# Residual sums joined to VectorE's written order in a convolution-and-attention block, and one softmax sum moved from GpSimd to VectorE

## The chip, the cores and the metric

The kernel runs on one core of a Trainium2 chip. The metric is the device time of one execution in microseconds (us), of which the median over the runs is taken. TensorE (PE in the profile) multiplies matrices, VectorE (DVE) and ScalarE (ACT) do elementwise work, GpSimd (POOL) a part of it, and SyncE (SP) issues the DMAs. Each engine works through its own instructions strictly in the order of the program, and waits where an operand or a buffer is not ready.

## The reference

Eight images of 512 channels and 32x32 positions, all in fp32. `cbs` is a convolution, a batch norm with given statistics and SiLU; `gn` is a group norm with 32 groups.

```python
def block(x):                                  # C = 256 channels, 4 heads of 64
    t = cbs(x, cv1)                            # 1x1, 512 -> 512
    ys = [t[:, :C], t[:, C:]]
    for i in range(2):
        yi = ys[-1]
        z = cbs(yi, m_cv1[i], 3x3)             # 256 -> 256
        z = bot_attention(z, m_qkv[i], rw[i], rh[i])   # over all 1024 positions
        z = silu(bn(conv1x1(z, m_cv2[i])))     # 256 -> 256
        ys.append(yi + z)
    return cbs(concatenate(ys), cv2)           # 1x1, 1024 -> 512

x = x + block(gn(x))
x = x + last(gn(x))      # 1x1, 512 -> 512; weights scaled, masked and permuted by group tables
```

The attention is a softmax of `q . (k + r) / 8` with `r` the sum of two learned position terms, and the weighted sum of `v`.

## The kernel before

**Data.** A tile has 128 partitions; an image's 256 channels are two such tiles, and its 1024 positions two halves of 512. Activations between stages go through DRAM: `y_dram[n][0..3]` are the four parts that conv2 concatenates, `x2_dram[n]` is the image after the block's residual.

**The attention in units.** The work is cut into 16 slots (one image's block `i`), in the order image 0 block 0, image 1 block 0, image 0 block 1, image 1 block 1, and then the next two images. A slot has four units (`Unit`, 64 in all, called by image, block, pair of heads and half of the queries: the last one is 7_1_1_1). A unit works on eight tiles `t` of 128 keys for two heads, 128x1024 numbers each:

- `logits(t)`: TensorE makes the logits (L510) in two PSUM banks `lg`, ScalarE copies them to SBUF as `st` (L517), and VectorE keeps the running maximum `mx` out of the banks (L522). A bank is free for another product when both are done.
- `top` and `spread`: the maximum over the keys, transposed and negated (L531) and spread again over PSUM (`mb`, L539).
- `soften(t)`: VectorE adds `mb` to `st` (L544, 128x1024).
- `exponent(t)`: ScalarE takes the exponential of `st` in place (L548). From `t` = 1 on, GpSimd adds it to the sum of exponentials `sum_...` in four parts of 128x256 (L555).
- `values(t)`: TensorE multiplies the exponentials by `v` into `po` (L562).
- `finish` and `divide`: TensorE sums `sum_...` over the partitions (`den`, L576), ScalarE copies it (L579), VectorE takes the reciprocal (L583) and scales `po` into `q` (L585).

While one unit takes its exponentials and weighted sums, the next one's logits are made.

**Filler.** Between the steps of the units a generator (`slot_filler`) emits all other work of that time in pieces: `conv3` (the 3x3 convolution as six row products on transformed rows, `plane` tiles, L313), `project` (q, k, v), `conv_m2` (the 1x1 convolution behind the attention), and, from a list `bg` of items, `conv1`, `conv2` and `last` of other images. Its matmuls have L175 (`accumulate`). The emission keeps a clock of estimated time, `Clock`: `clock.at(delay, f)` calls `f` when that clock has moved on by `delay`; group norms and row transforms are placed with it.

**Order.** The order of emission becomes the order of an engine only where an instruction goes through `in_turn` (VectorE), `act_turn` (ScalarE) or `pe_turn` (TensorE); each ties the instruction to the one before it in its chain. VectorE's chain holds the maxima, the softens and some of the row transforms. The rest, the residual sums among them, is placed by the framework's scheduler where it finds room. DMAs are issued by SP (`load`, L78).

**The residual sums.** `conv_m2` works on the halves `h` and, in each, on two output tiles `co`, and so makes four sums a call, here called add 1 to add 4. For each half it loads the residual (`res`, 512 KB) from `y_dram`, makes the product, ScalarE applies batch norm and SiLU (`m2s`, L130), VectorE adds (L430) and SP stores the sum to `y_dram`. For block 0 the sum is written into `ybuf`, the input of the next 3x3 convolution; for block 1 in place. `conv2` does the same for four output tiles of each half: SiLU (`cv2s`), add to the image's `x` (`xr`, L457), statistics of the group norm (L139), and after every second one a store to `x2_dram`. The residual tiles of `conv_m2`, `conv2` and `last` (`res`, `xr`, `x2r`) come from one pool, `gr`, with two buffers; the SiLU outputs from `tp` with three. The PSUM banks of all these products and of the logits are five (`ps_f`).

The group norm of `x2` ends in small ops on 128x4 numbers: `gm_b` and `gv_b` on TensorE (L146, L156), `gd_b` on VectorE (L150 to L152), `gr_b` on GpSimd (L160), and then it is applied by ScalarE (L165) to the tiles that `last` reads.

Of the kernel before, what the change touches and what calls it, by code (L numbers as in the profile page):

```python
# [17 lines left out]
ALU = mybir.AluOpType  # L18
# [7 lines left out]
IT = 2  # L26
F = 32
HW = F * F
HALF = 512
# [10 lines left out]
def conv_preact_kernel(ctx: ExitStack, tc: tile.TileContext, x, cv1, cv2, mcv1, qkv, mcv2, bn, rw, rh, conv, s_in, t_in, out):  # L40
    nc = tc.nc
# [23 lines left out]
    def pair(p, tag, name):  # L65
        return p.tile([P, 2, HALF], F32, tag=tag, name=name)

    def bank(name):
        return ps_f.tile([P, HALF], F32, tag="bank", name=name)

    def half_tile(name):
        return tp.tile([P, HALF], F32, tag="t", name=name)

    def flat(t):
        return t.rearrange("p a b -> p (a b)")

    def load(dst, src):
        nc.sync.dma_start(out=dst, in_=src)  # L78

    def weights(name, shape, src):  # L80
        t = wp.tile([P, *shape], F32, tag="w", name=name)
        load(t, src)
        return t
# [12 lines left out]
    y_dram = [[dram.tile([P, IT, HW], F32, name=f"y_{n}_{j}") for j in range(4)] for n in range(NB)]  # L96
    x2_dram = [dram.tile([P, 2, CT, HALF], F32, name=f"x2_{n}") for n in range(NB)]
# [24 lines left out]
    def y_rows(c, h):  # L122

        return ybuf[:, c, 1 + 16 * h : 17 + 16 * h].rearrange("p r x -> p (r x)")
# [4 lines left out]
    def bn_silu(dst, src, col):  # L129
        nc.scalar.activation(dst, src, AF.Silu, bias=bn_b[:, col : col + 1], scale=bn_s[:, col : col + 1])  # L130


    class GroupNorm:
        def __init__(self, name):
            self.name = name
            self.st = small.tile([P, CT, 2, 6], F32, tag="st", bufs=3, name=f"st_{name}")
# [34 lines left out]
    def accumulate(ps, terms):  # L171


        for n, (w, moving) in enumerate(terms):
            nc.tensor.matmul(ps, w, moving, start=(n == 0), stop=(n == len(terms) - 1))  # L175
            if n % 2 and n < len(terms) - 1:
                yield 1.72
        return Whole(1.72)
# [3 lines left out]
    def in_turn(instruction):  # L182

        if turn:
            tc.add_manual_dep(instruction.ins, turn.pop().ins.name, IN_ORDER, reason="order of VectorE")
        turn.append(instruction)

    def act_turn(instruction):

        if act_last:  # L190
            tc.add_manual_dep(instruction.ins, act_last.pop().ins.name, IN_ORDER, reason="order of ScalarE")
        act_last.append(instruction)
# [11 lines left out]
    class Spread:  # L204
# [7 lines left out]
        def upto(self, n):  # L212
            while self.done < n:
                self.done += 1
                in_turn(self.ops[self.done - 1]())

    class Image:
        def __init__(self, n):
            self.n = n
# [196 lines left out]
        def conv_m2(self, i):  # L416
            n = self.n
            name = f"{n}_{i}"
            w = weights(f"w_m2_{name}", (IT, 256), mcv2[i])
            q = self.q  # L420
            for h in range(2):
                res = pair(gr, "gr", f"res_{name}_{h}")
                load(res, y_dram[n][1 + i][:, :, ts(h, HALF)])
                for co in range(IT):
                    ps = bank(f"m2_{name}_{co}_{h}")
                    us = yield from accumulate(ps, [(w[:, c, ts(co, P)], q[:, c, ts(h, HALF)]) for c in range(IT)])
                    t = half_tile(f"m2s_{name}_{co}_{h}")
                    bn_silu(t, ps, BN_M2 + IT * i + co)
                    dst = y_rows(co, h) if i == 0 else res[:, co]
                    nc.vector.tensor_tensor(dst, res[:, co], t, ALU.add)  # L430
                    load(y_dram[n][2 + i][:, co, ts(h, HALF)], dst)
                    yield us


# [8 lines left out]
        def conv2(self, h, ys):  # L443
            n = self.n
            if h == 0:
                self.gn1 = GroupNorm(f"b{n}")
            for cp in range(2):
                res = pair(gr, "gr", f"xr_{n}_{h}_{cp}")
                load(res, x[n, cp, :, :, ts(h, HALF)])
                for c in range(2):  # L450
                    co = 2 * cp + c
                    w = weights(f"w_cv2_{n}_{h}_{co}", (2 * CT, P), cv2[co])
                    ps = bank(f"cv2_{n}_{h}_{co}")
                    us = yield from accumulate(ps, [(w[:, k], ys[k // 2][:, k % 2]) for k in range(2 * CT)])
                    t = half_tile(f"cv2s_{n}_{h}_{co}")
                    bn_silu(t, ps, BN_CV2 + co)
                    nc.vector.tensor_tensor(res[:, c], res[:, c], t, ALU.add)  # L457
                    self.gn1.stats(co, h, res[:, c])
                    if c == 0:
                        yield us  # L460
                load(x2_dram[n][:, h, 2 * cp : 2 * cp + 2], res)
                yield us


        def load_x2(self, h):
# [27 lines left out]
    class Unit:  # L493
# [52 lines left out]
        def exponent(self, t):  # L546
            st = flat(self.st[t])
            act_turn(nc.scalar.activation(st, st, AF.Exp))  # L548
            if t == 1:
                self.acc = pair(one, "acc", f"sum_{self.name}")  # L550
            for j in range(4 if t else 0):

                part = slice(256 * j, 256 * j + 256)
                so_far = self.st[0] if t == 1 else self.acc
                nc.gpsimd.tensor_tensor(flat(self.acc)[:, part], flat(so_far)[:, part], st[:, part], ALU.add)  # L555
# [185 lines left out]
    units = [Unit(im, i, hp, half) for im, i in slots for hp in range(IT) for half in range(2)]  # L741

    class Clock:
# [18 lines left out]
        def flush(self):  # L762
            for _, f in sorted(self.due, key=lambda d: d[0]):
                f()
            self.due.clear()

    clock = Clock()
# [81 lines left out]
    class Background:  # L849
# [5 lines left out]
        def add(self, *items):  # L855
            self.items += items
# [294 lines left out]
```

## Time and profile before

| | |
|---|---|
| time, three runs | 3152.05, 3156.82, 3157.03 us; median 3156.82 us |
| the profiled execution | 3162.82 us, of which 3161.1 us are the span from the first to the last instruction |
| granted TensorE clock, mean | 0.996 of full speed |
| TensorE's waits for other engines, largest entry | 16.2 us, 14 times (weighted sum for an exponential) |
| VectorE's waits, largest entry | 433.2 us, 174 times (maximum for ScalarE's copy) |
| GpSimd's waits, largest entry | 1336.5 us, 287 times (sum for an exponential) |
| residual loads of `conv_m2` | 32 of 512 KB, median 4.0 us from issue to landing |

In the profile a line of a group reads: code line, engine, operation, output tile <- input tiles, shapes, count | busy time in us, mean ns of one | idle time of the engine ahead of them, and what ended it. A line of the timeline reads: start and duration in us, engine, code line, operation, tiles, shapes, count of instructions drawn together; in brackets the idle time before and what ended it. A line of the waits reads: who waited for whom, the total in us, how many times, the longest in us. A matmul of 128x512 in fp32 has two records on PE of about 0.43 us each.

### The profile page before, as it was taken

The page shows a single profiled execution, that of the slowest core. Times are in us where ns is not written, and L with a number is a line of the kernel's source. Part 1 is how long each engine was busy: PE and PEld are TensorE (multiplying, and loading weights), DVE is VectorE, ACT ScalarE, POOL GpSimd, SP SyncE. Part 2 cuts the span into 40 slices and gives each one's busy share as a digit, 9 for nine tenths or more (in the row PEclk, how much of TensorE's full clock was granted, in tenths as well). Part 3 has the DMA queues.
Part 4 walks back from the last instruction along what each step waited for, and adds up shares of the span by engine and source line. Part 5 has one row for each costly group of instructions (what it writes and reads, how often), then busy time and mean ns, then how long its engine had stood idle before and what let it go on. Part 6 is the DMA issues. An engine that isn't in the chain of part 4 may idle for free.

```text
span 3161.1 us, 34185 instructions
## 1 busy us (share of the span) xinstructions
PE 3077.0 (97%) x11668; PEld 1515.3 (48%) x11668; DVE 2049.9 (65%) x2718; ACT 1721.0 (54%) x2349; POOL 1398.4 (44%) x1867
## 2 busy tenths in 40 slices
PE   7999999998999999999999999999999999999999
PEld 3645354454445454455445454454445454453333
DVE  5446577567667576667666676767666676767642
ACT  3245765855655555644656455544656455546621
POOL 2104444546444554455444454445444464444520
PEclk9999999999999999999999999999999999999999
DMA  8852352421233232424233332424233332413356
GB/s 289 292 182 74 130 180 87 153 77 63 88 116 131 79 128 71 149 84 148 84 116 130 114 127 70 153 85 136 91 110 130 120 120 70 150 64 120 120 205 217
DMA packets 142014, 399.35 MB, mean 126 GB/s; under 512 B 13072, under 2 KB 14352, under 8 KB 141840
## 3 DMA queue, kind: packets, MB, share of 16 engines
q1 hardware_dynamic: 141120, 396.94, 36.6%
q8 instruction: 92, 1.51, 0.2%
q14 instruction: 82, 0.67, 0.1%
q10 hardware_dynamic: 720, 0.23, 0.0%
HBM read 317.42 MB, written 79.69 MB: 126 GB/s over the span
## 4 chain that ended last, share of the span: by engine, by line
PE 75%; DVE 4%; ACT 4%; issue 2%; DMA 1%; POOL 1%; SPq 0%; ACTq 0%; DVEq 0%; POOLq 0%
PE cv L175 15%; PE m L313 13%; PE po L562 12%; PE lg L510 12%; PE l L175 7%; PE qk L175 6%; PE v L405 3%; PE m L175 3%; PE den L576 2%; PE mb L539 2%; PE mt L530 1%; ACT st L517 1%; DVE st L544 1%; ACT st L548 1%; DVE mx L522 1%
## 5 line engine op out<-in xcount | busy, mean ns | idle before, releaser
L555 POOL TENSOR_TENSOR sum<-sum,st 128x256 f32<-128x256 f32 x1536 | 1132.0, 771 | 552.1 <-ACT st L548 547.7
L522 DVE TENSOR_TENSOR mx<-mx,lg 128x512 f32<-128x512 f32 x768 | 477.8, 682 | 417.6 <-ACT st L517 417.4
L517 ACT COPY st<-lg 128x512 f32<-128x512 f32 x1024 | 525.0, 597 | 356.1 <-PE lg L510 331.7
L548 ACT ACTIVATE st<-st 128x1024 f32<-128x1024 f32 x512 | 539.1, 1068 | 304.1 <-DVE st L544 302.9
L544 DVE TENSOR_TENSOR st<-st,mb 128x1024 f32<-128x1024 f32 x512 | 604.4, 1215 | 60.2 <-PE mb L539 60.2
L555 POOL TENSOR_TENSOR sum<-st,st 128x256 f32<-128x256 f32 x256 | 185.1, 754 | 788.8 <-ACT st L548 788.8
L313 PE MATMUL m<-plane,w_m 128*128 128x256 f32 x2304 | 528.8, 383 | 4.9 <-ACT cv2s L130 2.7
L562 PE MATMUL po<-st,v 128*64 128x512 f32 x2048 | 497.8, 605 | 18.2 <-ACT st L548 16.2
L510 PE MATMUL lg<-q,k 64*128 64x512 f32 x2048 | 510.9, 617 | 2.9 <-ACT y L130 2.9
L313 PEld LDWEIGHTS m<-plane,w_m 128*128 128x128 f32 x2304 | 426.4, 189 | 129.5 <-issue 45.1
L175 PE MATMUL cv<-y,w_cv 128*128 128x512 f32 x1024 | 464.5, 599 | 7.9 <-ACT cv2s L130 4.6
L510 PEld LDWEIGHTS lg<-q,k 64*128 64x128 f32 x2048 | 177.3, 186 | 328.2 <-issue 267.4
L175 PEld LDWEIGHTS cv<-y,w_cv 128*128 128x128 f32 x1024 | 185.8, 190 | 248.1 <-issue 226.4
L562 PEld LDWEIGHTS po<-st,v 128*64 128x64 f32 x2048 | 128.8, 136 | 323.6 <-issue 237.3
L175 PE MATMUL cv<-x,w_cv 128*128 128x512 f32 x512 | 237.0, 610 | 10.6 <-ACT y L130 3.7
L175 PE MATMUL l<-x,w_l 128*128 128x512 f32 x512 | 236.9, 606 | 7.9 <-DVE mx L522 6.9
L175 PE MATMUL qk<-z,w_qkv 128*128 128x512 f32 x512 | 234.0, 600 | 1.4 <-DVE mx L522 1.4
L583 DVE RECIPROCAL rb<-rb 128x256 f32<-128x256 f32 x128 | 215.5, 1723 | 26.0 <-ACT rb L579 25.8
L531 DVE TENSOR_REDUCE nm<-mt 128x4 f32<-128x512 f32 x128 | 82.3, 684 | 144.7 <-PE mt L530 144.7
L579 ACT COPY rb<-den 128x512 f32<-128x512 f32 x64 | 37.3, 583 | 230.4 <-PE den L576 230.4
L175 PEld LDWEIGHTS cv<-x,w_cv 128*128 128x128 f32 x512 | 95.3, 194 | 132.0 <-issue 109.3
L175 PEld LDWEIGHTS l<-x,w_l 128*128 128x128 f32 x512 | 93.4, 191 | 130.4 <-issue 112.2
(145 smaller groups left out, 2408.8 us busy)
## 6 DMA issues: line engine op xcount, KB each, us to landing
w_m<-w_m SPq DMA_DIRECT2D x96, 768.0 KB, 4.8
w_cv<-in_cv SPq DMA_DIRECT2D x90, 512.0 KB, 3.5
y<-y SPq DMA_DIRECT2D x64, 512.0 KB, 4.8
x<-in_x SPq DMA_DIRECT2D x56, 512.0 KB, 5.2
y<-y SPq DMA_DIRECT2D x64, 256.0 KB, 3.5
k<-r SPq DMA_DIRECT2D x32, 512.0 KB, 3.6
res<-y SPq DMA_DIRECT2D x32, 512.0 KB, 4.0
xr<-in_x SPq DMA_DIRECT2D x32, 512.0 KB, 4.1
```

The source lines that it names most:

```text
L175: nc.tensor.matmul(ps, w, moving, start=(n == 0), stop=(n == len(terms) - 1))
L313: nc.tensor.matmul(ps[:, ts(co, 256)].rearrange("p (t x) -> p t x", x=F), w[:, co, c, dx], u[:, 9 * c : 9 * c + 8, dx : dx + F], start=(j ...
L405: nc.tensor.matmul(ps[:, ts(j, P)], z[:, c, ts(4 * j4 + j, P)], w[:, c, 512 + P * hp : 512 + P * hp + P], start=(c == 0), stop=(c == IT - 1),)
L510: nc.tensor.matmul(lg[h], self.k[r, ts(t, P)], self.q[r, self.hp, ts(self.half, HALF)], start=True, stop=True)
L517: act_turn(nc.scalar.copy(st[:, h], lg[h]))
L522: in_turn(nc.vector.tensor_tensor(self.mx[:, h], so_far[:, h], lg[h], ALU.max))
L531: nc.vector.tensor_reduce(self.nm[:, h], mt, AX.X, ALU.max, negate=True)
L544: in_turn(nc.vector.tensor_tensor(st, st, flat(self.mb), ALU.add))
L548: act_turn(nc.scalar.activation(st, st, AF.Exp))
L555: nc.gpsimd.tensor_tensor(flat(self.acc)[:, part], flat(so_far)[:, part], st[:, part], ALU.add)
L562: nc.tensor.matmul(self.po[HD * h : HD * h + HD], self.v[:, t, ts(h, HD)], self.st[t][:, h], start=(t == 0), stop=(t == KT - 1),)
L583: nc.vector.reciprocal(self.rb[:, r], self.rb[:, r])
```

## The change

Three edits, and a helper class.

- `Later(delay)`: `add(f)` puts a function in a queue and asks the clock to run the queue up to it after `delay`; `flush()` runs what is left.
- `conv_m2`: the residual add and the store of its result are emitted through `Later(2.0)`, and the add goes through `in_turn`, so that it has a place in VectorE's chain. The queue is flushed with the last tile.
- `conv2`: the same with `Later(3.0)`; the add is in the chain, and the group norm's statistics and the store to `x2_dram` are emitted with it. One more `yield` is in the place of the one behind the store.
- `Unit.exponent`: for the last unit the sums of exponentials are seven VectorE adds of 128x1024 in the chain, in place of 28 GpSimd adds of 128x256.

```diff
+    class Later:
+        def __init__(self, delay):
+            self.delay, self.waiting = delay, []
+        def add(self, f):
+            self.waiting.append(f)
+            clock.at(self.delay, lambda: self.upto(f))
+        def upto(self, f):
+            while f in self.waiting:
+                self.waiting.pop(0)()
+        def flush(self):
+            if self.waiting:
+                self.upto(self.waiting[-1])
...
     conv_m2:
+            later = Later(2.0)
...
-                    nc.vector.tensor_tensor(dst, res[:, co], t, ALU.add)
-                    load(y_dram[n][2 + i][:, co, ts(h, HALF)], dst)
+                    def add(h=h, co=co, dst=dst, src=res[:, co], t=t):
+                        in_turn(nc.vector.tensor_tensor(dst, src, t, ALU.add))
+                        load(y_dram[n][2 + i][:, co, ts(h, HALF)], dst)
+                    later.add(add)
+                    if (h, co) == (1, IT - 1):
+                        later.flush()
                     yield us
...
     conv2:
+            later = Later(3.0)
...
-                    nc.vector.tensor_tensor(res[:, c], res[:, c], t, ALU.add)
-                    self.gn1.stats(co, h, res[:, c])
-                    if c == 0:
-                        yield us
-                load(x2_dram[n][:, h, 2 * cp : 2 * cp + 2], res)
-                yield us
+                    def add(cp=cp, c=c, co=co, res=res, t=t):
+                        in_turn(nc.vector.tensor_tensor(res[:, c], res[:, c], t, ALU.add))
+                        self.gn1.stats(co, h, res[:, c])
+                        if c == 1:
+                            load(x2_dram[n][:, h, 2 * cp : 2 * cp + 2], res)
+                    later.add(add)
+                    if (cp, c) == (1, 1):
+                        later.flush()
+                    yield us
...
     Unit.exponent:
+            if t and self is units[-1]:
+                so_far = self.st[0] if t == 1 else self.acc
+                in_turn(nc.vector.tensor_tensor(flat(self.acc), flat(so_far), st, ALU.add))
+                return
             for j in range(4 if t else 0):
```

## The prediction

> **What bounds the kernel now.** I read the page first, then TensorE's waits, then VectorE's groups of L430, then the timeline at the places that the change touches.
>
> ```profile
> PE 3077.0 (97%) x11668; PEld 1515.3 (48%) x11668; DVE 2049.9 (65%) x2718; ACT 1721.0 (54%) x2349; POOL 1398.4 (44%) x1867
> ```
>
> TensorE is busy for 3077.0 us of a span of 3161.1 us. Only 84 us can be won by any reordering, and a stall of TensorE anywhere is lost for good. Its waits, longest in total first:
>
> ```profile
> PE po L562 <- ACT st L548: 16.2, 14, 3.7
> ...
> PE gv_b L156 <- DVE gd_b L152: 5.9, 1, 5.9
> PE cv L175 <- ACT cv2s L130: 4.6, 6, 0.8
> ```
>
> So the weighted sums (po) wait now and then for an exponential, one group norm near the end waits 5.9 us in one piece, and conv2 waits a little for its own SiLU (cv2s), because its PSUM bank is freed late. VectorE's adds of the residual, and what they wait for (last column: idle time before them):
>
> ```profile
> L430 DVE TENSOR_TENSOR ybuf<-res,m2s 128x512 f32<-128x512 f32 x32 | 28.2, 902 | 27.0 <-ACT m2s L130 17.8 <-DMA res<-y 9.1
> L430 DVE TENSOR_TENSOR res<-res,m2s 128x512 f32<-128x512 f32 x32 | 27.0, 870 | 9.5 <-DMA res<-y 6.2 <-ACT m2s L130 3.2
> ```
>
> VectorE waits only 15.3 us in all (9.1 + 6.2) for residual tiles to land. These adds are outside the written order of VectorE, so the scheduler could put softens (L544) and running maxima (L522) in front of an add whose tile was late.
>
> **The change: the chain.** Now every residual add is emitted some 2 or 3 us later and joined to VectorE's written order. The order of the built program shows what that does: the add stands at the place where it is emitted, with later softens and maxima behind it, whatever its tile does. Most adds find their tile there and cost nothing: conv2's tiles (xr) are loaded a whole conv2 tile ahead, and the second block of images 0, 2 and 4 uses two different buffers. The pool gr has two buffers, though. Where conv2 holds one of them, conv_m2's second-half tile must take the buffer of its first half; its load then leaves only when adds 1 and 2 are done (for the second block also their store, which reads that buffer). Adds 3 and 4 stand in the chain directly behind add 2, so VectorE stands still for the load. That happens in three kinds of place, in three images each.
>
> Kind A, conv_m2 of the second block of images 1, 3, 5 (near 985, 1695, 2404 us):
>
> ```profile
> 982.62 2.35 DVE L544 TENSOR_TENSOR st<-st,mb 128x1024 f32<-128x1024 f32 x2
> 984.88 1.23 DVE L430 TENSOR_TENSOR res<-res,m2s 128x512 f32<-128x512 f32 x1
> 988.49 0.52 SPq L78 DMA_DIRECT2D res<-y  x1
> 991.40 1.22 DVE L544 TENSOR_TENSOR st<-st,mb 128x1024 f32<-128x1024 f32 x1
> 992.52 1.94 PE L562 MATMUL po<-st,v 128*64 128x512 f32 x8
> 992.53 2.10 DVE L430 TENSOR_TENSOR res<-res,m2s 128x512 f32<-128x512 f32 x2
> ```
>
> Before, softens 2 and 3 ran at 982.62, then add 2, and the load (issued 988.49, 3.9 us to landing) was covered by four maxima and soften 4. In the new order the sequence is add 2, add 3, add 4, soften 2, soften 3, maxima. Step by step: add 2 ends about 985.9; its store has to be read out, so the load leaves 2.35 us later (986.14 to 988.49 before), at 988.25, and lands at 992.15. Adds 3 and 4 (0.69 each) end at 993.55, soften 2 at 994.75, exponential 2 (1.06) at 995.85. The weighted sum that began at 992.52 begins at 995.9, 3.4 us late. ScalarE then has four PSUM copies (2.03) in front of exponential 3, which ends at 998.95; its weighted sum, the second four of the eight records, began at 993.49 before and now begins at 999.0: 5.5 us late, and the next logits are behind it on TensorE. **3 x 5.5 = 16.5 us.** Bounds: 3.4 (only the first wait counts) and 7.6 (5.5 and 2.1 for a slow clock, below).
>
> Kind B, conv_m2 of the first block of images 2, 4, 6 (near 1117, 1825, 2534):
>
> ```profile
> 1131.37 1.82 DVE L430 TENSOR_TENSOR ybuf<-res,m2s 128x512 f32<-128x512 f32 x2
> ...
> 1137.70 0.72 DVE L282 TENSOR_TENSOR plane<-a,b 128x544 f32<-128x544 f32 x1
> ...
> 1139.89 5.45 PE L313 MATMUL m<-plane,w_m 128*128 128x256 f32 x24 [0.91 <-ACT cv2s L130]
> ```
>
> The load left at 1125.93 and took 5.3 us; it now stands ahead of a load of w_m on SP's queue, so it lands at 1130.0 (its median 4.0) to 1131.2. Behind adds 3 and 4 (1.4) the order now has softens 4 and 5 (2.35, before at 1121.26), four maxima (2.48, before at 1128.97), the plane's ops a and b (1.44), softens 6 and 7 (2.35), conv2's add (0.73) and the plane (0.72): 11.5 us, so it ends at 1141.5 to 1142.7, and the product that began at 1139.89 starts 1.6 to 2.8 us late. **3 x 2 = 6 us**, bounds 0 (absorbed) and 4.
>
> Kind C, conv_m2 of the first block of images 3, 5, 7 (near 1298, 2006, 2714):
>
> ```profile
> 1299.82 0.52 SPq L78 DMA_DIRECT2D res<-y  x1
> 1302.41 3.70 PE L175 MATMUL cv<-y,w_cv 128*128 128x512 f32 x8 [0.60 <-DVE mx L522]
> 1307.08 0.69 DVE L430 TENSOR_TENSOR ybuf<-res,m2s 128x512 f32<-128x512 f32 x1 [3.52 <-DMA res<-y]
> 1316.01 1.98 PE L175 MATMUL l<-x,w_l 128*128 128x512 f32 x4 [2.48 <-DVE mx L522]
> ```
>
> Add 3 already waited 3.52 us for a load of 7.2 us, but three of the four maxima had gone ahead, at 1301.67; they free the PSUM banks, and conv2 at 1302.41 was waiting for the first of them. Now all four are behind add 3. On SP's queue the two loads of x2 and one of w_m, issued at 1301.85 to 1304.43, stand behind the store of add 3, so they no longer compete with the residual's load: it lands after 5.0 to 7.2 us, at 1304.9 to 1307.1, and the first maximum ends 1.4 us later, at 1306.3 to 1308.4. conv2 is 3.9 to 6 us late. The later x2 loads make their two group-norm activations, which are ahead of the next exponential on ScalarE, equally late, and `l` at 1316.01 goes to 1320 or 1321. **3 x 5 = 15 us**, bounds 2 (a late conv2 swallows the 2.48 us wait) and 6.5.
>
> Sum of the stalls: 37.5 us, with bounds 3 x 5.4 = 16 and 3 x 18.1 = 54.
>
> The TensorE clock could add to it. In the tail below, the matmuls after 5.9 us of idling run at half rate (eight records in 5.76 us instead of 3.70), a loss of 2.1 us; after a wait of 3.72 us at 2888.24 po's eight records took 3.31 us instead of 1.94; after idling 3.07 us at 1312.94 there was none. The waits worked out above (3.4, 2, 4 to 5) lie in between; I take nothing in the middle and 2.1 in the upper bounds of A (for C it is in the 6.5). [...]
>
> **Small edits.** The y store and the x2 store move with their adds by at most a few us; their readers come tens of us later. The conv2 SiLU stands before an exponential on ScalarE in places where TensorE waited 0.6 to 0.9 us for it: 3 x 0.9 = **2.7 us won**, bounds 0 and 4.6 (that whole row of waits).
>
> **The last unit's sums.** 28 POOL adds go; seven VectorE adds of 128x1024 come, at about 1.2 us each (the soften of the same size takes 1.215).
>
> ```profile
> 3009.41 16.46 POOL L555 TENSOR_TENSOR sum<-sum,st 128x256 f32<-128x256 f32 x24 [1.20 <-ACT st L548]
> 3016.98 8.90 DVE L150 TENSOR_TENSOR gd_b<-mv_b,gms_b 128x4 f32<-128x4 f32 x1
> 3026.33 0.59 PE L156 MATMUL gv_b<-gd_b,gmat 128*128 128x4 f32 x2 [5.90 <-DVE gd_b L152]
> 3026.78 5.76 PE L175 MATMUL l<-x,w_l 128*128 128x512 f32 x8
> ```
>
> A subtraction of 128x4, 0.16 us elsewhere, lasts 8.90 us and ends with POOL's run of sums, and TensorE waits for it. Without that run it takes 0.16 us. In the new order I put sums and softens one after another from 3004.9: softens 2 and 3 end at 3010.7, sums 2 and 3 at 14.0, softens 4 and 5 at 16.4, sums 4 and 5 with the residual of `last` at 19.5, and between the three small gd ops stand softens 6 and 7, so gd is ready at 3023.3 and not 3026.3: 3.0 us. The idle time falls from 5.9 to 2.9 us, nearest to the 3.07 that was followed by full rate, so 2.0 more are won on the next eight records: **5 us**, bounds 3 and 6.
>
> [...]
>
> **Sum.** 37.5 - 2.7 - 5 = +29.8 us. The profiled execution took 3162.8 us (span 3161.1 and 1.7 around it), 6.0 above the median of 3156.8. So 3192.6 beside the former, and 3186.6 beside the median: about 0.9% slower.
>
> **The rivals.** Measurement can tell about 0.2% (6.3 us) from no change.
> 1. Faster (0.15): the loads land before VectorE reaches add 3, and only the gains are left. For kind A that needs add 3 to begin by 988.7, so that soften 2 and exponential 2 end at 992.5: the load would have to leave by 984.8, before add 2 has even run. Against it: the two buffers and the 2.35 us of the store. For it: 84 us of TensorE's idle time could take up part of a stall. Price: -2.7 - 5 = -7.7, about 3149.
> 2. No change (0.07): stalls of 1 us at each of the nine places, taken up by waits that were there anyway: +9 - 7.7, about 3158.
> 3. Slower, and by more than I forecast (0.08): each of A and C also brings the half-rate clock, and nothing is won at the tail: 37.5 + 6 x 2.1 = +50, about 3207.
> 4. The forecast (0.70): 3186.6.
>
> The bounds of the sum, 16 - 4.6 - 6 = +5 and 54 - 3 = +51, give 3162 to 3208 for the likeliest case and the third; with the second the range reaches down to 3155, and what is left out is mostly the first. Faster 0.15, same 0.08, slower 0.77.
>
> **What would show it.** In the profile after: TensorE's waits for exponentials (16.2 us before) grow by some 15 us, and its waits for maxima by some 10; VectorE's idle time before the residual adds for `DMA res<-y` grows from 15.3 to about 40 us; at about 992 an add with a wait of several us stands before softens 2 and 3; the conv2 product of kind C waits 4 us or more; POOL's 24 sums near 3010 and the 8.90 us subtraction are gone and gv_b waits 3 us. I am wrong if the waits for `DMA res<-y` do not grow, or if they grow and TensorE's idle time does not.

## The result, and the profile after

The changed kernel takes 3207.04 us (median of 5 runs, 3205.93 to 3210.36) against 3154.26 us before (5 runs in the same session): the ratio is 1.0163, with a 95% interval of 1.0151 to 1.0174, so some 51 us were lost where 30 were forecast. The sign, the kind of place and the range were right; the size was not, and the time lies only 1 us inside the upper end of the range (3208). The profiled execution of the changed kernel took 3207.04 us, with a span of 3205.3 us and a mean granted clock of 0.991 (0.996 before). Its engines, on the page:

```profile
PE 3098.5 (97%) x11668; PEld 1519.9 (47%) x11668; DVE 2041.9 (64%) x2725; ACT 1719.0 (54%) x2347; POOL 1373.0 (43%) x1839
```

TensorE has the same 11668 records as before and is busy for 21.5 us longer (3098.5 against 3077.0). Its idle time grew by 22.7 us (106.8 against 84.1). So half of the longer span is waiting. Of the other half the slow clock accounts for a part: by the profile's record of the granted clock TensorE was at half rate for 29.7 us before and for 56.7 us now, and it worked in 23.9 and 48.8 us of these. With half of that working time counted as lost, 12.0 and 24.4 us, the slow clock makes about 12.5 us of the 21.5, an estimate from the 0.5 in that record (at the first place of A, below, four records of po took 1.98 us at half rate and 1.08 at full); the rest is not taken apart here. TensorE's waits (total, times, longest):

```profile
PE po L598 <- ACT st L579: 24.2, 14, 3.7
PE cv L175 <- DVE mx L553: 14.0, 6, 3.0
...
PE m L331 <- ACT st L548: 8.6, 3, 2.9
...
PE qk L175 <- DVE mx L553: 4.5, 7, 1.6
```

These four are kind A, kind C, kind B and one that the forecast did not have; before, the first, second and fourth were 16.2, 4.1 and 1.4 us, and the third was not among the entries, which go down to 0.3. VectorE's residual adds, with the idle time before them in the last column:

```profile
L451 DVE TENSOR_TENSOR ybuf<-res,m2s 128x512 f32<-128x512 f32 x32 | 26.5, 846 | 49.4 <-ACT m2s L130 26.6 <-DMA res<-y 14.5 <-ACT st L548 8.3
L451 DVE TENSOR_TENSOR res<-res,m2s 128x512 f32<-128x512 f32 x32 | 24.8, 801 | 45.6 <-DMA res<-y 25.6 <-ACT m2s L130 19.9
```

The waits for `DMA res<-y` went from 15.3 to 40.1 us, as the forecast asked. Of the other signs, the row of po grew by 8.0 us and not by some 15, and TensorE's waits for maxima by 12 in all, where some 10 were forecast. Kind A in the timeline (start and duration; idle time in brackets):

```profile
989.14 0.52 SPq L78 DMA_DIRECT2D res<-y  x1
...
993.26 1.29 DVE L451 TENSOR_TENSOR res<-res,m2s 128x512 f32<-128x512 f32 x2 [6.54 <-DMA res<-y]
...
994.48 2.34 DVE L575 TENSOR_TENSOR st<-st,mb 128x1024 f32<-128x1024 f32 x2
...
996.83 1.98 PE L598 MATMUL po<-st,v 128*64 128x512 f32 x4 [3.61 <-ACT st L579]
...
999.72 1.98 PE L598 MATMUL po<-st,v 128*64 128x512 f32 x4 [0.92 <-ACT st L579]
...
1001.63 2.95 PE L541 MATMUL lg<-q,k 64*128 64x512 f32 x8
```

VectorE stands still for 6.54 us in front of add 3, and then softens 2 and 3 follow. TensorE waits 3.61 and 0.92 us. The four records of po between the two waits take 1.98 us, where four such records behind a wait take 1.08 at full rate (below), and eight records of the logits 2.95 and not 1.99: that is the slow clock. Kind C:

```profile
1310.61 0.52 SPq L78 DMA_DIRECT2D res<-y  x1
...
1315.65 0.69 DVE L451 TENSOR_TENSOR ybuf<-res,m2s 128x512 f32<-128x512 f32 x1 [2.81 <-ACT st L548]
...
1316.99 5.40 PE L175 MATMUL cv<-y,w_cv 128*128 128x512 f32 x8 [2.97 <-DVE mx L553]
```

The profile puts add 3's wait down to ScalarE's copies, but these ended at 1314.74. The load took 5.0 us, from 1310.61 to 1315.6, and that is when the add starts. This conv2 waited 0.60 us before and now waits 2.97 us (the forecast's sign was 4 or more), and its eight records take 5.40 us, not 3.70.

Kind B and the tail:

```profile
1137.59 1.29 DVE L451 TENSOR_TENSOR ybuf<-res,m2s 128x512 f32<-128x512 f32 x2 [4.82 <-DMA res<-y]
...
1150.03 2.57 PE L331 MATMUL m<-plane,w_m 128*128 128x256 f32 x6 [2.84 <-ACT st L548]
```

```profile
3069.37 0.15 DVE L150 TENSOR_TENSOR gd_b<-mv_b,gms_b 128x4 f32<-128x4 f32 x1
...
3071.98 0.39 PE L156 MATMUL gv_b<-gd_b,gmat 128*128 128x4 f32 x2 [1.67 <-DVE gd_b L152]
3072.23 3.68 PE L175 MATMUL l<-x,w_l 128*128 128x512 f32 x8
```

In kind B VectorE waits 4.82 us for the load, and the product waits 2.84 us; it begins 0.1 us after the plane that it reads, which began at 1148.68 and took 1.24 us. Measured against conv2's product ahead of it (1128.06 before, 1136.27 now), it begins 1.9 us late. In the tail the subtraction takes 0.15 us, gv_b waits 1.67 us, and the records behind it run at full rate (3.68).

The granted clock at the places, by stretches (from and to, length, then for PE, PEld, DVE, ACT and POOL the busy time in us and the records; the last three numbers are the granted TensorE clock, the share of the DMA engines and GB/s). The rows are the first place of kind A, the three of kind B and the first of kind C:

```profile
987.00:1017.00 30.00, 25.47 (x92) 13.40 (x91) 16.72 (x22) 17.66 (x23) 13.86 (x20) 0.89 0.31 104
1127.00:1157.00 30.00, 27.16 (x87) 13.23 (x86) 22.68 (x29) 18.71 (x25) 19.86 (x24) 0.94 0.53 175
1309.00:1345.00 36.00, 31.58 (x95) 13.41 (x94) 25.29 (x34) 23.74 (x31) 18.47 (x24) 0.95 0.60 204
...
1851.00:1881.00 30.00, 27.06 (x94) 12.59 (x93) 23.41 (x30) 20.12 (x27) 20.06 (x25) 1.00 0.53 174
...
2580.00:2610.00 30.00, 27.19 (x94) 13.99 (x93) 22.38 (x29) 17.93 (x23) 19.83 (x24) 0.94 0.55 179
```

The clock is 0.89, 0.89 and 0.83 in the three stretches of A, and 0.95, 0.91 and 0.95 in those of C. Before, it was 1.00 in all nine but the third of C, which had 0.95. In this profile's record of the granted clock the half rate came at these places in pieces of 3.41, 6.83 and 10.24 us.

**Where the time went.** For each matmul I took its start in the changed profile less its start in the profile of before, and from that lag the jump over each kind of place (medians of the matmuls behind it less those ahead), summed over three images. The same was done for the experiments below. The column "product 0 twice" is the run in which the whole product is made a second time. The last row leaves out the start-up, which differs by a few us between executions.

```
us, 3 places each        forecast  changed  adds 3,4  product  small tiles,  small tiles,
                                            free      0 twice  chain kept    conv2 out
kind A                     16.5      23.8     -0.3      17.9      -0.3          -0.3
kind B                      6.0       9.2     10.4      10.8      -0.6          -2.9
kind C                     15.0      15.9     16.2      14.0      11.6           6.0
tail (last unit)           -5.0      -6.5     -6.4      -6.3      -5.3          -6.7
all, from 170 us on        29.8      46.5     29.5      46.6       6.5          -2.0
```

### The profile page after: what moved, and what is told of

It is laid out like the page before. It is cut to its first block, busy times and chain, and to the rows that moved or that the text cites. A ratio compares the mean times of both kernels' runs of the same rounds, so it can differ in the third digit from the quotient of the medians.

```text
span 3205.3 us, 34148 instructions
## 1 busy us (share of the span) xinstructions
PE 3098.5 (97%) x11668; PEld 1519.9 (47%) x11668; DVE 2041.9 (64%) x2725; ACT 1719.0 (54%) x2347; POOL 1373.0 (43%) x1839
## 5 line engine op out<-in xcount | busy, mean ns | idle before, releaser
L591 POOL TENSOR_TENSOR sum<-sum,st 128x256 f32<-128x256 f32 x1512 | 1108.5, 767 | 605.5 <-ACT st L579 599.7
L598 PE MATMUL po<-st,v 128*64 128x512 f32 x2048 | 509.1, 608 | 32.9 <-ACT st L579 24.2
L175 PEld LDWEIGHTS qk<-z,w_qkv 128*128 128x128 f32 x512 | 92.4, 190 | 131.4 <-issue 96.7
```

What stands on the lines that cost most here:

```text
L598: nc.tensor.matmul(self.po[HD * h : HD * h + HD], self.v[:, t, ts(h, HD)], self.st[t][:, h], start=(t == 0), stop=(t == KT - 1),)
```

## The experiments

My theory was that VectorE stands still in its chain for the residual load. The rivals were that the place of the adds ahead of the softens costs by itself, that the later emission with its stores costs, and that one of the other edits is behind the loss.

**One edit alone, three times.** Each kernel is the one before with one of the three edits as in the diff.

Only the last unit's sums:

> Only the last unit's sums of exponentials go to VectorE; everything else is the kernel before. The lag of TensorE between the two traces fell by 6.2 us around the last unit and rose by 1.4 us behind it. If this edit alone is behind that: 4 to 6 us faster than before, the 8.90 us subtraction is gone, and gv_b waits 1 to 3 us. Rival (the 8.90 us are not POOL's doing): within 1 us of before.

Measured: 0.9994 (0.9985 to 1.0003), 3159.64 against 3160.73 us. The profile has the tail 7.2 us shorter, with the subtraction at 0.15 us. The times alone can't tell the gain from nothing.

Only conv2's edit:

> Only conv2's edit. My theory puts the loss on conv_m2's adds alone, since conv2's tiles are loaded early: TensorE's waits of conv2 for cv2s go (about 0.8 us at three places), and the time is 0 to 3 us below before. Rival (any residual add placed in the chain in front of softens and maxima costs): 64 adds of 0.8 us in front of softens, of which a half would count: 10 to 25 us slower.

Measured: 1.0031 (1.0019 to 1.0042), 10 us slower by the ratio: the lower end of the rival, and not the gain that I expected. The tail is 5.3 us shorter, but kinds B and C each lose over 4 us, and a new wait appears in this kernel as in the changed one:

```profile
PE qk L175 <- DVE mx L546: 4.8, 7, 1.9
PE m L331 <- DVE x2r L510: 4.7, 3, 1.9
```

A conv2 add in the chain waits for its SiLU (in the changed kernel VectorE is idle for 132.2 us in all ahead of these 64 adds until `ACT cv2s`, against 125.0 before), and the softens and maxima behind it wait too; so do adds outside the chain that come after them, such as that of `last` (x2r), which frees a PSUM bank. My theory missed this: a chained op need not wait for a load to hold the chain up.

Only conv_m2's edit:

> Only conv_m2's edit. My theory: the whole loss and a bit more, since the two gains are left out: 50 to 58 us slower than before, with the nine jumps of the lag near 985, 1117, 1298 us and their two repetitions. Rival (the loss is shared between both chains): 20 to 35 us slower.

Measured: 1.0184 (1.0165 to 1.0202), 58 us by the ratio: the whole loss, with the jumps of A at 25.6 us. The three ratios together (0.9994, 1.0031 and 1.0184) make 66 us where the change has 51. The gap is in truth wider by 5 to 7 us, for the gain at the tail is in two of the three kernels and can be had once only. Most of it is at B and C: conv_m2's edit has 28.1 us there by itself, more than the whole change (25.1), and conv2's some 9 more, so the waits of the two chains cover each other.

**Half of conv_m2's adds out of the chain.**

```diff
-                        in_turn(nc.vector.tensor_tensor(dst, src, t, ALU.add))
+                        ins = nc.vector.tensor_tensor(dst, src, t, ALU.add)
+                        if h == 0:        # the other kernel: h == 1
+                            in_turn(ins)
```

> The changed kernel, but of conv_m2's four adds only the first two go through VectorE's chain; adds 3 and 4, which wait for the second load, are placed by the scheduler. In the built order kind A is back to softens first, kind B half, kind C still has add 3 in front of its maxima. My theory (the load wait inside the chain): the three jumps of kind A (7.5 to 8.4 us of lag each) go, those of C stay, so 20 to 30 us of the 50 go and the kernel is 20 to 30 us slower than before. Rival (the place of adds 1 and 2, or the later stores, is the cost): 45 to 55 us slower, as the change itself.

Measured: 1.0096 (1.008 to 1.0111), 30 us by the ratio. Kind A is gone (23.8 to -0.3), and the time falls by 21 us. B and C are as they were, for there adds 3 and 4 still run ahead of the maxima and wait for their load, as at the first place of B:

```profile
1135.71 2.09 DVE L451 TENSOR_TENSOR ybuf<-res,m2s 128x512 f32<-128x512 f32 x2 [2.54 <-DMA res<-y]
1137.73 2.47 DVE L555 TENSOR_TENSOR mx<-mx,lg 128x512 f32<-128x512 f32 x4
```

So this run tests kind A alone.

> The opposite: adds 3 and 4 in the chain, adds 1 and 2 placed by the scheduler. In the built order kind A and B are as in the changed kernel and kind C has softens 2 and 3 ahead of adds 1 and 2, add 3 still ahead of the maxima. My theory: the jumps stay, 40 to 52 us slower than before. Rival (the place of adds 1 and 2): under 25 us slower.

Measured: 1.0165 (1.0148 to 1.0183), the same as the change, with A at 24.3 us. So in kind A it is adds 3 and 4, those behind the second load, and not adds 1 and 2.

**Later, but out of the chain.** Both `in_turn` calls around the residual adds are taken away; `Later` stays.

> The changed kernel with both kinds of residual adds still emitted later, and their stores with them, but out of VectorE's chain. My theory (the chain costs, not the delay): the jumps are gone, within 5 us of before, perhaps some us below it through the tail. Rival (the later emission with its stores and loads behind it costs): 20 us or more slower than before.

Measured: 1.0036 (1.0023 to 1.0048), 11 us slower by the ratio, between my theory and the rival. Its profiled execution, 3166.04 us, was the fastest of its five, and has A at 1.4, B at 1.7 and C at 4.2 us. So the chain makes some 40 of the 51 us; the later emission has a price as well, which I don't resolve further.

**The load early, the chain kept.** This is the test that I trust most. A third buffer of the full size does not fit into SBUF (the pool `wt` needs 6.375 KB of a partition, and 2.5625 KB would be left). So the pool `gr` holds five tiles of 128x512, and residuals are loaded and stored in such halves; adds 2, 3 and 4 still stand ahead of softens 2 and 3 in kind A.

```diff
-    gr = pool("gr", 2)
+    gr = pool("gr", 5)
...
-                res = pair(gr, "gr", f"res_{name}_{h}")
-                load(res, y_dram[n][1 + i][:, :, ts(h, HALF)])
+                res = [gr_half(f"res_{name}_{h}_{co}") for co in range(IT)]
+                for co in range(IT):
+                    load(res[co], y_dram[n][1 + i][:, co, ts(h, HALF)])
```

(the same in `conv2` and `last`; `gr_half` makes a tile of 128x512; four tiles of the start-up are moved to other pools)

> The changed kernel with the same chain on VectorE, but the pool gr holds five tiles of 128x512 (256 KB) instead of two of 128x2x512, and every residual is loaded and stored in such halves; four small start-up tiles moved to buffers that are idle then to make room. In the built order adds 2, 3 and 4 still stand ahead of softens 2 and 3 in kind A, but their tiles are asked for before add 1. My theory (VectorE stands still for the load): its idle time for the residual load falls from 40 us to under 10, the jumps of kind A (7.5 to 8.4 us) fall under 2, and the kernel is 0 to 15 us slower than before. Rival (the place of the adds ahead of the softens): 35 us or more slower than before.

Measured: 1.0032 (1.0021 to 1.0043). The groups of the adds, and kind A's place:

```profile
L455 DVE TENSOR_TENSOR ybuf<-res,m2s 128x512 f32<-128x512 f32 x32 | 27.7, 891 | 32.4 <-ACT m2s L133 32.4
L455 DVE TENSOR_TENSOR res<-res,m2s 128x512 f32<-128x512 f32 x32 | 24.6, 798 | 21.6 <-ACT m2s L133 21.6
```

```profile
982.07 2.48 DVE L455 TENSOR_TENSOR res<-res,m2s 128x512 f32<-128x512 f32 x3 [2.11 <-ACT m2s L133]
...
984.48 2.34 DVE L580 TENSOR_TENSOR st<-st,mb 128x1024 f32<-128x1024 f32 x2
...
989.77 1.94 PE L603 MATMUL po<-st,v 128*64 128x512 f32 x8
```

No wait for a load is left. Three adds run one after another, the softens follow at once, and po comes without a wait, in eight records at full rate. A and B are gone with the order unchanged: the theory is shown there, and the control below has the same tiles without the chain. Kind C is not: of 15.9 us, 11.6 stay.

The control, the kernel before with the same tiles, and then with the last unit's sums added:

> The control: the kernel before with the same tiles of 128x512. If the smaller transfers cost or win something by themselves, it shows here. My theory: in kind C add 3 no longer waits 3.52 us and conv2 not 0.6 us; 0 to 6 us faster than before. Rival (twice as many DMAs for the same bytes hold SP up): 5 us or more slower.

Measured: 0.9986 (0.9977 to 0.9994); C is 5.5 us shorter, 0 us of waiting for `DMA res<-y`.

> The kernel before with the tiles of 128x512 and the last unit's sums on VectorE: the two parts that should help. My theory: the gains add up, 4 to 12 us faster than before. Rival: one of them is not there, within 3 us of before.

Measured: 0.9971 (0.996 to 0.9982), 3150.03 against 3159.56 us. This version beats both kernels.

**What is left of kind C.** The small tiles, conv_m2's adds in the chain, conv2's out of it.

> The changed kernel with the tiles of 128x512 (no load wait left), and conv2's adds out of VectorE's chain; conv_m2's adds stay in it. What is left of kind C without the load wait (11.6 us in three places) has two candidates: a wait of 1.9 us of a row product for the residual add of last, which conv2's chained add and the softens behind it hold up, and a wait of 1.7 us of po for an exponential that stands behind the group norm of x2 on ScalarE. In the built order the first is as in the kernel before and the second stays. If conv2's chain is the first: kind C falls from 11.6 to 4 to 7 us, the five waits of 0.75 us in the qk products go too, and the time is 6 to 12 us below that of the same kernel with conv2 in the chain (within 4 us of before). Rival (all that is left is conv_m2's order): kind C stays above 9 us, and the time at 8 to 11 us above before.

Measured: 1.0007 (0.9996 to 1.0019), 8 us less by the two ratios, and C at 6.0 us. So conv2's chain makes 5.6 us of C. What stays beside the 1.86 us wait of po, which this profile still shows for an exponential behind the group norm of x2, wasn't taken apart.

**The clock.** In images 3, 5 and 7, row product 0 of block 0 is made a second time, in one kernel its second half alone, in another the whole of it:

```diff
-                for co in range(IT):
+                twice = (r, i) == (0, 0) and n in (3, 5, 7)
+                for rep, co in enumerate((0, 1, 1) if twice else range(IT)):   # the other kernel: (0, 1, 0, 1)
...
```

> The changed kernel with extra work that changes no result: in images 3, 5 and 7 the second half of row product 0 of block 0 is computed twice, so TensorE has 2.6 us more to do at the three places of kind A, inside its wait for exponential 2; no other engine's order changes. If the half-rate clock after the idle time is a part of the cost: po and the logits behind the wait run at full rate, the jump of the lag at each place falls from about 8 to 5 to 6 us, and the time is 5 to 9 us below that of the changed kernel (42 to 46 us above before), although there is more work. Rival (the idle time alone is the cost): the jumps stay within 0.5 us, or grow.

Measured: 1.0179 (1.0165 to 1.0193), jumps of 9.0, 9.0 and 7.7 us: the forecast of my theory failed. The timeline says why:

```profile
1002.18 1.08 PE L599 MATMUL po<-st,v 128*64 128x512 f32 x4 [1.42 <-ACT st L580]
1005.07 1.98 PE L599 MATMUL po<-st,v 128*64 128x512 f32 x4 [1.81 <-ACT st L580]
1006.98 3.79 PE L542 MATMUL lg<-q,k 64*128 64x512 f32 x8
```

The wait was cut in two, 1.42 and 1.81 us with 1.08 us of work between, and the half rate came all the same, only later. So this run did not take the slow clock away. The second one did:

> The changed kernel, with row product 0 of block 0 computed twice in whole in images 3, 5, 7: 5.2 us of added TensorE work at each of the three places of kind A, so that TensorE waits well under 1 us in all there (when half of the product was repeated it still waited 1.4 and 1.9 us and ran at half rate). If the half-rate clock is a part of the cost: no half-rate po or logits behind the wait, the jump falls from about 8 to 5 to 6.5 us, and the time is 4 to 9 us below the changed kernel. Rival (the clock has no part in it): the jumps are as before or larger by the added work.

```profile
1002.31 1.08 PE L599 MATMUL po<-st,v 128*64 128x512 f32 x4
1004.19 1.08 PE L599 MATMUL po<-st,v 128*64 128x512 f32 x4 [0.80 <-ACT st L580]
1005.20 1.99 PE L542 MATMUL lg<-q,k 64*128 64x512 f32 x8
```

Measured: 1.0146 (1.0132 to 1.0159). With 5.2 us more work at each place, po and the logits run at full rate and the jumps fall to 6.1, 6.0 and 5.9 us. Idle time alone does not explain this; the clock is part of the cost, at least 1.4 to 2.5 us a place.

Single waits elsewhere do not sort by their length. In the kernel before, a wait of 2.13 us had the half rate behind it (16 records of this shape took 7.13 us at 1128.06):

```profile
609.73 8.83 PE L175 MATMUL cv<-x,w_cv 128*128 128x512 f32 x16 [2.13 <-ACT m2s L130]
```

With the last unit's sums alone, a wait of 3.72 us had full rate behind it, and with the adds out of the chain one of 3.81 us:

```profile
2890.07 2.02 PE L567 MATMUL po<-st,v 128*64 128x512 f32 x8 [3.72 <-ACT st L548]
```

```profile
1319.68 1.98 PE L175 MATMUL l<-x,w_l 128*128 128x512 f32 x4 [3.81 <-DVE mx L553]
```

## Why the prediction was right or wrong, step by step

- **The chain and the load (A, B, part of C).** Right in place, order and mechanism; taking away the load wait with the order kept took away A and B. In A the predicted idle time was 5.5 us (3.4 and 2.1); measured were 4.5 (3.61 and 0.92), because the four slow records between the waits take 0.9 us off the second.
- **The term that failed: the TensorE clock, taken at nothing.** I chose by the nearest row to the longest wait, and misread it: the 3.07 us at 1312.94 run from the start of one record to the start of the next, and the idle time in the row is 2.48 us. The profile of before also has a shorter wait, of 2.13 us, with the half rate behind it, which I overlooked. Measured in A, two times 1.98 us for 1.08 and 2.95 for 1.99 make 2.8 us at the first place, and in C 5.40 for 3.70 makes 1.7. By the granted clock, with half of the working time at half rate counted as lost, A has 9.4 us, B 3.1 and C 5.0 (net of 1.7 before), against 12.6 for A and C in the third rival. Over the whole span it is the 12.5 us above, and the forecast beside its own profile, 3192.6 us, is 14.4 us short. Without the load wait the half rate lasted 18.8 us in all, not 56.7. The longest single wait is no safe test: the half rate came behind two waits of 1.42 and 1.81 us with work between them, and behind the one of 2.13 us, while full rate followed one of 3.72 us with the last unit's sums alone, and one of 3.81 us with the adds out of the chain. What decides was not shown.
- **Kind B.** Forecast 6, measured 9.2 us. The product was 1.9 us late, inside the forecast 1.6 to 2.8. The clock, which halved at the first and the third place (0.94) and not at the second (1.00), took 3.1 us, and that makes up what is above the forecast.
- **Kind C.** Forecast 15, measured 15.9 us, but the step was only in part the cause, and that the two agree is in part luck. The first conv2 was 3.4 us late, less than the forecast 3.9 to 6, and some 5 of the 15.9 us are the clock, for which the forecast had nothing. Without the load wait 11.6 us stay: other waits ran beside it. 5.6 of them are conv2's chain.
- **"Most adds find their tile there and cost nothing."** Wrong for conv2: its edit alone costs 10 us by the ratio, though its tail gains 5. The qk waits (1.4 to 4.5 us) and the adds of `last` behind it had no term. Near 430 us a further 4.6 us went, 2.4 of them given back at 607; it is gone with the small tiles.
- **cv2s: -2.7 us.** Measured -0.8, -0.8 and -0.6, so -2.2 in all.
- **The tail: -5 us.** Measured -6.5, and the row of 8.90 us went: the wait fell from 5.90 to 1.67 us and the eight records behind it from 5.76 to 3.68, where 3.0 and 2.0 were forecast. But moving the sums is not the only way: with conv2's edit alone or the small tiles alone POOL's run stayed, and the subtraction took 0.25 and 0.34 us. And in the times the edit alone can't be told from nothing.
- **The reference point.** The sum was made against a profiled execution of 3162.82 us and carried over to the median. The changed kernel's profile stood at its median, before's 6 to 9 us above its own. So the two profiles are 44 us apart and the medians 53; the difference is not a part of the change that I could point to.
- **The rivals.** The loads did not come early, and nothing was absorbed. What came is nearest to the third, forecast plus slow clock, at 3207 us, to which I had given 0.08; but the gain at the tail, which it left out, was there. The time lies inside the range only because its upper end carried slow clocks in A and C, which the sum did not.

## What to carry to other kernels

An op that is tied into an engine's written order takes its operand's latest arrival with it (6.54 us of VectorE at the first place of A): before chaining it, see when its buffer comes free, not only when its data are made, and move the load (more, smaller buffers) rather than the op. Price a new stall of TensorE with the slow clock behind it, as something that may or may not come (here it came behind 2.13 us and not behind 3.81), and count short waits close together as one (it came behind 1.42 and 1.81 us with 1.08 us of work between). Parts of a change that wait side by side must be taken away one after another, since each hides the others.

## What the runs showed of the hardware

Small VectorE ops next to a run of POOL sums, in the kernel with conv2's edit alone (POOL's sums first, then the three small ops):

```profile
3021.86 16.48 POOL L579 TENSOR_TENSOR sum<-sum,st 128x256 f32<-128x256 f32 x24 [2.91 <-ACT st L572]
```

```profile
3028.56 0.25 DVE L150 TENSOR_TENSOR gd_b<-mv_b,gms_b 128x4 f32<-128x4 f32 x1
...
3028.84 0.65 DVE L151 TENSOR_TENSOR gd_b<-gd_b 128x4 f32<-128x4 f32 x1
...
3029.52 0.65 DVE L152 TENSOR_TENSOR gd_b<-gd_b,mv_b 128x4 f32<-128x4 f32 x1
```

Each ends 0.02 us after the POOL sum that was running when it began, and none lasted longer than one sum (0.69 us). In the kernel before and in that with conv_m2's edit alone the measurement differs: the first of these ops lasted 8.90 and 8.85 us there, through the rest of POOL's run. In these two kernels it began 0.03 and 0.08 us after a POOL sum had begun, and 0.40 and 0.50 us after in the two kernels with POOL's run where it passed. But the second and third op, which passed too, began only 0.09 to 0.10 us after a sum had begun. What decides is open; no run tried it.
